# Layer 1's weight factors parked one sum a pair by GpSimd's queue, and another order in the last quad

## The chip, the cores and the metric

The kernel runs on one core of a Trainium2 chip. The metric is the time of one execution on the device, in microseconds; a measurement is the median of several executions. A profiled execution has a span (first to last instruction) beside its own time. The engines are TensorE (PE, with its weight loads PEld), VectorE (DVE), ScalarE (ACT), GpSimd (POOL) and SyncE (SP). Each takes its instructions in the order in which they were built. SP computes nothing here: it issues most of the DMAs; GpSimd issues others and does some elementwise work.

## The reference

A batch of 128 graphs, each with 128 nodes of 512 features, goes through two layers in float32, each of the form x + layer(relu(layernorm(x))).

```python
# layer 0: h = relu(layernorm(x))
Xw = X @ Wv + bv
e = leaky_relu(sj[:, None, :] + si[:, :, None] + ab[0])      # sj, si: Xw times the halves of aw
alpha = A * exp(e)
transition = alpha / (sum(alpha, -1) + 1e-12)
for k in range(3):
    H = H + Xk @ Wk[k] + bk[k]
    Xk = transition @ Xk
return relu(H)
# layer 1: h = relu(layernorm(x))
q, k = split(X @ Wqk);  v = X @ Wv
w = mask / sqrt(512) * sum(q * (adj @ (k * mask)), -1)
return softmax(w, axis=1)[:, :, None] * v
```

Layer 1 needs no q and k of its own: the product of the two halves of Wqk is formed once, so that its score is a product of h, a 512x512 matrix and the aggregate adj @ h. With Wv beside it, its weight is a matrix of 512x1024.

## The kernel before

**Tiling.** The graphs are taken in pairs, p = 0 to 63, in layer 0, and in quads (two pairs), q = 0 to 31, in layer 1. All large products use Strassen's scheme with seven products instead of eight: layer 0 once, layer 1 twice (outer and inner). Its form here (`strassen`, `one_round`) runs products 1, 5, 6, 2, 7, 3, 4 on four PSUM banks a, b, c, e; between them ScalarE copies a to b, e to s, b to c and c to s, and VectorE adds the banks to s. `y10` multiplies by the first two weights of layer 0, `y2` by the third; `inner` and `outer` apply the transition matrix.

**Weight factors.** Layer 1's weight matrix enters as seven outer factors, in the order FACTORS = 1, 5, 2, 6, 3, 7, 4, and each of these as seven inner ones: three are blocks of the outer factor, four are sums, made one from the other. In pairs 5 to 8 `combine_steps(*OUTER)` makes the outer sums, one a pair, each 128x1024. From FIRST = 9 on, `prepare` (lines 653 to 663) makes one factor a pair: four sums of 128x256 on VectorE into the tile `stage`, two ahead of the pair's `begin` and two in the middle of `statistics`, then four stores to the array `rwd` in DRAM, issued by SP behind the store of x1: one with the four sums (512 KB), three with the blocks (128 KB each). After pair 16 the room of the factors' sources (`prep`, `stage`) is given up; the first four factors are read back into it, one a pair, 896 KB each, by SP. The other three are read at the start of layer 1.

**A pair of layer 0.** While PE runs `y10` of pair p and `y2` of pair p + 2, the other engines prepare what comes. SP issues, in order: the store of h (hd) and its read back in blocks (hv), the store of x1 (x1d), the load of x for pair p + 4 (xg), the store of the transition matrix (td) and of the second norm's h (h2d), the read back of td in blocks (junk), and that of h2d (hv). VectorE turns the blocks into transposes: x from hv<-hd, tt from junk, fw from hv<-h2d (line 431). After those follow the pair's x1 (line 625) and its statistics (line 294), then ScalarE's Ln and Exp for it. Behind Exp (`issue_after` of "ln") ScalarE copies y2's first block, then s<-c. GpSimd issues pzd and pz (a column of y2 spread over all partitions through DRAM), fd (the transposed blocks and their sums, 1 MB), and four agb (the adjacency in blocks).

**The order on an engine.** `behind(what, op)` builds `op` so that it stands behind the instruction noted as `done[what]`; `ordered` does that for PE's matmuls. In layer 1 `put` keeps a chain for each engine in the order of the calls.

**The last quad** has its order written by hand in `steps(...)`. The rounds are ra (factors 1 and 2, banks set1), rb (6 and 7, set2), r4 (set1), r5 (set2) and r3 (set1); `(rb, 2)` is rb's third product, p6, with its copy b to c. The others are p1 (0), p5 (1), p2 (3), p7 (4), p3 (5), p4 (6). The tiles s1 and s2 hold the copies of p5. `c[:, 0..3]` are the quad's outputs: scores of the two pairs in 2 and 0, values in 1 and 3. `score` multiplies an aggregate by an output and sums (a SCALAR_TENSOR_TENSOR into junk), `spread_columns_of` turns the scores by PE and takes their maximum (`peaks`), `exp_own` and `exp` form the exponentials on ScalarE, `factors` the quotient, `scale` multiplies the values of an earlier quad, `add_x1` adds x1 to them by a DMA of GpSimd's, `finish` makes the last output and stores it. `p5_of_r5` adds r5's p5 to values 3 and 1 on GpSimd.

Of the kernel before, what the change touches and what calls it, by code (L numbers as in the profile page):

```python
# [9 lines left out]
FP = mybir.dt.float32  # L10
# [6 lines left out]
def kernel(  # L17
# [25 lines left out]
    nc = tc.nc  # L43
# [39 lines left out]
    def behind(what, op, *args, **how):  # L83

        with tc.issue_after(done[what]):
            return op(*args, **how)  # L86
# [6 lines left out]
    def bcast(ap, offset, n):  # L93

        return bass.AP(tensor=ap.tensor, offset=ap.offset + offset, ap=[[0, P], [1, n]])
# [355 lines left out]
    def y2(p, steps={}, gate=None, after="ln"):  # L451


        add = partial(behind, gate, nc.vector.tensor_add) if gate else nc.vector.tensor_add
        y = Y2[p] = front.tile([P, G, 2, WP], FP, name="y2")[:, :, :, :W2]
        s = front.tile([P, 2, WP * 2], FP, name="s", bufs=1)[:, :, :W2]

        def y00(a):
            done["y00"] = behind(after if gate else "warm", nc.scalar.copy, y[:, 0, 0], a).ins

        def y10(c):
            done["y10"] = nc.scalar.copy(y[:, 1, 0], c).ins

        strassen(set2, LEFT[p], right2, s, True, {
            (0, 0): y00,
            (1, 1): lambda e, t: add(y[:, 1, 1], e, t),
            (0, 1): lambda b, t: add(y[:, 0, 1], b, t),
            (1, 0): y10}, steps, seventh="y00")
        if p > 1:

            t = small.tile([P, G, S32], FP, name="pzt", bufs=1)
            behind(gate or "warm", nc.vector.transpose, t, y[:, :, 0, :S32])
            d = dram.tile([G, Q, S32], FP, name="pzd")
            nc.gpsimd.dma_start(d.rearrange("g q b -> q g b"), t[::S32])
            PZ[p] = front.tile([P, G, N], FP, name="pz")
            nc.gpsimd.dma_start(PZ[p].rearrange("p g n -> p (g n)"), bcast(d, 0, G * N))
        else:
            PZ[p] = a2[:, :G * N].rearrange("p (g n) -> p g n", g=G)

# [168 lines left out]
    RWD = {o: dram.tile([P, 7, HD], FP, name=f"rwd{o}", bufs=1) for o in FACTORS}  # L648

    FIRST = 1 + 2 * DC  # L650
    OUTER = ({(kh, k): rl[:, kh * HC:(kh + 1) * HC, k] for kh in range(2) for k in range(2)}, [tl[:, i] for i in range(4)])

    def prepare(o, stage):

        r = {(k, h): rightl[o][:, k, h * HD:(h + 1) * HD] for k in range(2) for h in range(2)}
        t = stage.tile([P, 4, HD], FP, name="stage")

        def store_all():
            behind("x1d", nc.sync.dma_start, RWD[o][:, :4], t)
            for i, at in enumerate(((0, 0), (1, 0), (1, 1))):  # L660
                behind("x1d", nc.sync.dma_start, RWD[o][:, 4 + i], r[at])

        return combine_steps(r, [t[:, i] for i in range(4)]), store_all

    INNER = {5: 0, 6: 1, 7: 2, 3: 3}
    RIGHT = {5: 0, 6: 1, 7: 2, 4: 3, 1: 4, 2: 5, 3: 6}
# [84 lines left out]
    for p in range(NP):  # L751
        weights, weights_end = [], None
        if DC < p <= 2 * DC:
            weights = combine_steps(*OUTER)[p - DC - 1:p - DC]
            weights_end = lambda: rightl.update(combined(*OUTER))
        elif FIRST <= p < FIRST + len(FACTORS):
            weights, weights_end = prepare(FACTORS[p - FIRST], stage)

        def between():
            if p == 0:  # L760
                behind("t", norm0, 2)
                behind("rs", begin, 1)
                return
            if len(weights) > 1:
                for step in weights[:2]:
                    behind("t", step)
            if p + 2 < NP:
                behind("right" if weights else "t", begin, p + 2)
            if p + 3 < NP:
                two = weights[-2:]  # L770
                RS0[p + 3] = behind("left", statistics, xg[p + 3],
                                    middle=(lambda: [behind("aggr", step) for step in two]) if two else None, last="right")

        if p == NP - 1:
            behind("rs2", attention, p)
        def norms():
            if p and p + 3 < NP:
                behind("s7", norm0, p + 3, RS0.pop(p + 3))

        steps = {1: between, 3: norms}  # L780
        if p in T:
            steps[2] = lambda: t_transposed(p)
        if p > 1:
            steps[5] = lambda: masked(p, "ba")
        y10(p, steps)
        if p > 0:
            behind("c12", for_layer1 if p < NP - 1 else SUMS.pop(NQ - 2), *([p - 1] if p < NP - 1 else []))
        if p == NP - 2:
            f0 = w2[:, :8 * G * HC * N].rearrange("p (o j k n) -> p o j k n", o=8, j=G, k=HC)
            load_left(0, swdge)  # L790
        if p == NP - 1:
            for step in inner_sums(0, FACTORS[:4]):
                behind("c12", step)
        z = inner(p)
        if p == 0:
            y2(1, {2: lambda: RS0.update({3: behind("left", statistics, xg[3], "u2")})})
            behind("y10", behind, "hv", norm0, 3, RS0.pop(3))
            spread_columns(1)
            attention(1, lambda: begin(2))
        behind("c12" if p else "left", outer, p, z)  # L800
        if weights:
            weights_end()
        if p + 4 < NP:
            load_x(p + 4)
        if 0 < p <= DC:
            behind("x1d", rows, rl[:, :, 1], wv1, (p - 1,))
        if p == 0:
            setup_ctx.close()
            left = layer0.enter_context(tc.tile_pool(name="left", bufs=1))
            stage_ctx = ExitStack()  # L810
            stage = stage_ctx.enter_context(tc.tile_pool(name="stage", bufs=2, side="right"))
        if p + 2 < NP:
            def ahead():
                attention_exp(p + 1, gate="aggr")
                attention_adj(p + 1)

            def statistics_and_ahead():
                norm2_statistics(p, middle=ahead)
                attention_t(p + 1, "rs2")
                t_by_blocks(p + 1)  # L820

            y2(p + 2, *(({2: statistics_and_ahead}, "t", "z") if p else ()))
        if p + 2 < NP:
            behind("s7", seed_a)
            behind("s7", seed_e)
        elif p + 1 < NP:
            seeds_last()
        norm2(p)
        if p + 3 < NP:
            load_adj(p + 3)  # L830
        if p == FIRST + len(FACTORS):
            stage_ctx.close()
            prep_ctx.close()
            early = ctx.enter_context(tc.tile_pool(name="early", bufs=1, side="right"))
            RW = {o: early.tile([P, 7, HD], FP, name=f"rw{o}") for o in FACTORS[:4]}
        if FIRST + len(FACTORS) <= p < FIRST + len(FACTORS) + 4:
            o = FACTORS[p - FIRST - len(FACTORS)]
            behind("x1d", nc.sync.dma_start, RW[o], RWD[o])
    def left1(q, o, i):
        if i in INNER:  # L840
            return IN[q, o][:, INNER[i]]
# [166 lines left out]
    def exp_own(v, pw, peak):  # L1008
        act(nc.scalar.activation, v[:, 4], v[:, 3], AF.Exp)

    def factors(v, pw, peak):
        dve(nc.vector.reciprocal, v[:, 5], v[:, 2])
        dve(nc.vector.tensor_mul, v[:, 3], v[:, 4], v[:, 5])
# [259 lines left out]
    second_p5()  # L1273
    exp(*soft[2], 3)
    factors(*soft[2])
    exp_own(*soft[0])
    exp(*soft[0], 0)
    steps((rb, 2))
    exp(*soft[0], 1)
    scale(prior, 0, 0)  # L1280
    steps((rb, 3))
# [9 lines left out]
        to = c[:, 1::2, i, j]  # L1291
        return lambda bank, *t: dve(nc.vector.tensor_add, to, bank.to_broadcast([P, 2, HD]), to)

    def p5_of_r5():

        for k in (3, 1):
            pool(nc.gpsimd.tensor_add, c[:, k, :, 1], c[:, k, :, 1], s2[:, 0:1, :HD].to_broadcast([P, G, HD]))

    corners = ((0, 0), (1, 1), (0, 1), (1, 0))
    r4 = one_round(q, set1, (4,), s1, {at: on_s7(*at) for at in corners},  # L1300
                   early=lambda e: in_place(c[:, 0, :, 1])(e.to_broadcast([P, G, HD])))
    r5 = one_round(q, set2, (5,), s2, {at: both(*at) for at in corners}, direct=True)
    r3 = one_round(q, set1, (3,), s1, {at: in_place(c[:, 1:2, at[0], at[1]]) for at in corners},
                   early=lambda e: in_place(c[:, 1, :, 1])(e.to_broadcast([P, G, HD])))

# [4 lines left out]
            op0=OP.mult, op1=OP.add)  # L1310
        queue.dma_start(out[(2 * q + pair) * G + j], r)

    steps((r4, 0), (rb, 5))
    scale(prior, 1, 0)
    steps((r4, 2), (r4, 3), (rb, 6))
    scale(prior, 1, 1)
    add_x1(prior, 1)
    steps((r4, 4), (r5, 0), (r4, 5), (r5, 1), (r4, 1))
    score(1, 0, c[:, 0])
    steps((r4, 6), (r5, 2))  # L1320
    score(1, 1, c[:, 0])
    p5_of_r5()
    for pair in range(2):
        store(late, pair)
    for pair in range(2):
        store(prior, pair)
    steps((r5, 3), (r3, 0), (r5, 4), (r3, 1), (r5, 5))
    soft[1] = spread_columns_of(W[q], a2, G, G)
    exp_own(*soft[1])
    exp(*soft[1], 0)  # L1330
    steps((r3, 2), (r3, 3), (r5, 6))
    exp(*soft[1], 1)
    steps((r3, 4), (r3, 5))
    factors(*soft[1])
    finish(0, 0, c[:, 1, 0], nc.scalar)
# [29 lines left out]
```

## Time and profile before

| | |
|---|---|
| median of 3 executions | 2225.51 us (2223.95 to 2227.53) |
| the profiled execution | 2225.62 us, span 2223.8 us |
| DVE / ACT / POOL busy | 1668.8 / 1236.0 / 697.9 us |
| moved by DMA | 519.35 MB, mean 234 GB/s |
| layer 0, pairs 0 to 62 | about 36.6 to 1408 us of the span |
| last quad | from about 2186 us |

In the lines of the profile a group is named by its line, engine, operation and tiles (out<-in). L91, L86 and L673 are lines of helpers (`ordered`, `behind`, `put`), so that such a line covers many operations; the tiles tell them apart. DVE, ACT, POOL and PE rows are instructions of the engines; SPq and POOLq rows are issues of DMAs. In a timeline the columns are start and length in us, engine, line, operation, tiles, and in brackets the idle time ahead of it with what ended it. In a list of waits they are the waiting instruction, what it waited for, the total in us, the number of waits and the longest one. PE's granted clock was full, 1.00, in every window shown here up to the last few microseconds.

### The profile page before, as it was taken

The numbers are of one execution on the slowest core, as the hardware profiler recorded it, in microseconds if no ns is written. First come the engines' busy times: TensorE is split into PE (matmuls) and PEld (weight loads), VectorE is DVE, ScalarE is ACT, GpSimd is POOL, SyncE is SP. The second block draws the span as 40 slices with busy tenths as digits, with TensorE's granted clock in tenths as the row PEclk, the third lists the DMA queues.
The fourth block names the chain that finished last, engine by engine and source line by source line (L and its number), as shares of the span: only waits on it lengthen the run. The fifth ranks groups of instructions, "written<-read, shape, count | busy, mean of one in ns | idle before, by whom it ended". The sixth has DMA issues, their size and how long they took to land.

```text
span 2223.8 us, 29417 instructions
## 1 busy us (share of the span) xinstructions
PE 2204.0 (99%) x8113; PEld 1535.0 (69%) x8113; DVE 1668.8 (75%) x4532; ACT 1236.0 (56%) x2857; POOL 697.9 (31%) x821
## 2 busy tenths in 40 slices
PE   9999999999999999999999999999999999999998
PEld 6666655666666566666666666688788878887886
DVE  6778777778777777877878777587777767777777
ACT  4555454555455555555555454456666666666664
POOL 2112111212121121212111121255555554555554
PEclk9999999999999999999999999999999999999999
DMA  7688787898788787888778786768888888888876
GB/s 210 202 241 238 226 268 245 272 275 245 228 231 233 225 243 216 245 230 230 239 223 244 217 242 205 264 199 238 229 254 229 233 234 247 236 225 248 235 222 177
DMA packets 425743, 519.35 MB, mean 234 GB/s; under 512 B 100310, under 2 KB 281174, under 8 KB 409706
## 3 DMA queue, kind: packets, MB, share of 16 engines
q1 hardware_dynamic: 384152, 392.36, 58.4%
q0 software_dynamic: 41136, 124.57, 21.5%
q8 instruction: 65, 1.06, 0.2%
q14 instruction: 100, 0.82, 0.1%
q10 hardware_dynamic: 290, 0.53, 0.1%
HBM read 295.26 MB, written 222.07 MB: 233 GB/s over the span
## 4 chain that ended last, share of the span: by engine, by line
PE 90%; DMA 4%; DVE 4%; SPq 1%; issue 1%; ACT 1%; DVEq 0%; ACTq 0%
PE a L91 26%; PE c L91 24%; PE b L91 24%; PE e L91 15%; DMA td<-t 2%; DMA hv<-h2d 2%; SPq L538 1%; DVE st L294 1%; DVE fw L431 1%; SPq L346 0%; DVE x L625 0%; DVE z L86 0%; DMA h2d<-h 0%; DMA xg<-in_x_dram 0%; PE a L284 0%
## 5 line engine op out<-in xcount | busy, mean ns | idle before, releaser
L673 POOL TENSOR_TENSOR c<-s,c 128x512 f32<-128x512 f32 (+1 forms) x186 | 201.1, 1095 | 250.3 <-DVE s L673 245.2
L111 POOL DMA_DIRECT2D agb<-in_adj_dram x256 | 149.8, 592 | 338.3 <-DVE aT L86 246.9
L91 PE MATMUL a<-r,x 128*128 128x512 f32 x512 | 240.8, 592 | 0.0
L91 PE MATMUL b<-rw,in 128*128 128x256 f32 x884 | 212.0, 379 | 0.0
L91 PEld LDWEIGHTS b<-rw,in 128*128 128x128 f32 x884 | 168.0, 190 | 23.3 <-issue 0.5
L439 POOL DMA_DIRECT2D fd<-fw x62 | 34.7, 559 | 470.1 <-DVE fw L447 275.0
L91 PEld LDWEIGHTS a<-r,x 128*128 128x128 f32 x512 | 97.0, 190 | 95.7 <-issue 92.3
L86 ACT COPY s<-c 128x257 f32<-128x257 f32 (+1 forms) x128 | 61.5, 481 | 173.3 <-PE c L91 173.2
L86 ACT COPY b<-a 128x257 f32<-128x257 f32 (+1 forms) x128 | 59.3, 464 | 168.9 <-PE a L91 168.9
L86 DVE TENSOR_TENSOR e<-e,s 128x512 f32<-128x512 f32 x64 | 44.7, 698 | 142.6 <-ACT s L86 142.6
L673 POOL TENSOR_TENSOR c<-c 128x1024 f32<-128x1024 f32 x61 | 144.1, 2362 | 11.2 <-DVE c L673 10.8
L91 PE MATMUL a<-w,x 128*128 128x257 f32 x512 | 131.9, 380 | 0.1
L91 PE MATMUL b<-w,sx 128*128 128x257 f32 x512 | 132.0, 380 | 0.0
L91 PE MATMUL c<-t,sx 128*128 128x512 f32 x256 | 120.5, 593 | 0.2
L91 PE MATMUL e<-t,sx 128*128 128x512 f32 x256 | 120.3, 592 | 0.0
L91 PE MATMUL b<-t,sx 128*128 128x512 f32 x256 | 120.3, 592 | 0.0
L91 PE MATMUL c<-t,x 128*128 128x512 f32 x256 | 120.3, 592 | 0.0
L91 PE MATMUL b<-r,sx 128*128 128x512 f32 x256 | 120.3, 592 | 0.0
L673 DVE SCALAR_TENSOR_TENSOR junk<-agg,wscale,c 128x512 f32<-128x512 f32 x126 | 97.1, 770 | 29.8 <-POOL c L673 24.3
L673 ACT ACTIVATE c<-c,wcol 128x512 f32<-128x512 f32 x124 | 86.3, 720 | 55.7 <-DVE wcol L673 55.7
L431 DVE STREAM_TRANSPOSE fw<-hv 128x256 f32<-128x256 f32 x248 | 88.2, 413 | 34.2 <-DMA hv<-h2d 33.8
L91 PE MATMUL a<-rw,f 128*128 128x256 f32 x448 | 108.1, 379 | 0.0
(265 smaller groups left out, 5256.9 us busy)
## 6 DMA issues: line engine op xcount, KB each, us to landing
fd<-fw POOLq DMA_DIRECT2D x62, 1024.0 KB, 5.1
xg<-in_x_dram SPq DMA_DIRECT2D x64, 512.0 KB, 7.1
x1d<-x SPq DMA_DIRECT2D x64, 512.0 KB, 4.2
h2d<-h SPq DMA_DIRECT2D x64, 512.0 KB, 3.7
hd<-h SPq DMA_DIRECT2D x63, 512.0 KB, 3.6
hv<-hd SPq DMA_DIRECT2D x252, 128.0 KB, 3.9
hv<-h2d SPq DMA_DIRECT2D x248, 128.0 KB, 4.1
h<-h2d SPq DMA_DIRECT2D x62, 512.0 KB, 8.6
```

The source lines that it names most:

```text
L86: return op(*args, **how)
L91: done["mm"] = op(*args, **how).ins
L111: nc.gpsimd.dma_start(agb[p][c * S32:(c + 1) * S32].rearrange("p g q i -> p (g q) i"), v[c])
L294: nc.vector.bn_stats(st, src[:, j, :])
L431: done["c12"] = nc.vector.transpose(blocks[:, k, j].rearrange("p f (n b) -> p f n b", n=Q), hv[:, j].rearrange("p n (k f a) -> p k f n a", ...
L439: nc.gpsimd.dma_start(fd[:, half].rearrange("p o n -> p (o n)"), fv[:, half].rearrange("p o n -> p (o n)"))
L538: done["tv"] = nc.sync.dma_start(tv[c * S32:(c + 1) * S32].rearrange("p g q i -> p (g q) i"), v[c]).ins
L673: done[engine] = op(*args, **how).ins
```

## The change

The sums and stores of the weight factors are spread: each of pairs 9 to 36 makes one sum, in the middle of `statistics`, and stores it (128 KB) and, for three of four sums, one block (128 KB), on GpSimd's queue behind pz, after `y2` instead of behind `outer`. The room is given up after pair LAST = 37, and the first four factors are read back from there in 16 pieces of two inner factors or one, one piece a pair, by GpSimd's queue behind pz. `begin` of pairs 5 to 36 no longer stands behind the sums.

In the last quad: rb's p6 with its copy comes ahead of the exponentials of the first pair's scores; r5's p5 comes ahead of r4's p1 and puts its copy into s1 instead of s2; `p5_of_r5` is taken apart, value 1 ahead of `add_x1(prior, 1)`, value 3 behind r5's p6 and ahead of the last score; r3's p6 with its copy comes ahead of the second pair's exponentials, and r3's p2 and r5's p4 behind both of these.

```diff
             PZ[p] = front.tile([P, G, N], FP, name="pz")
-            nc.gpsimd.dma_start(PZ[p].rearrange("p g n -> p (g n)"), bcast(d, 0, G * N))
+            done["pzq"] = nc.gpsimd.dma_start(PZ[p].rearrange("p g n -> p (g n)"), bcast(d, 0, G * N)).ins
...
+    LAST = FIRST + 4 * len(FACTORS)
+    PIECES = [(o, slice(i, min(i + 2, 7))) for o in FACTORS[:4] for i in range(0, 7, 2)]
...
-    def prepare(o, stage):
+    STAGED = {}
+
+    def prepare(o, i, stage):
 
         r = {(k, h): rightl[o][:, k, h * HD:(h + 1) * HD] for k in range(2) for h in range(2)}
-        t = stage.tile([P, 4, HD], FP, name="stage")
-
-        def store_all():
-            behind("x1d", nc.sync.dma_start, RWD[o][:, :4], t)
-            for i, at in enumerate(((0, 0), (1, 0), (1, 1))):
-                behind("x1d", nc.sync.dma_start, RWD[o][:, 4 + i], r[at])
-
-        return combine_steps(r, [t[:, i] for i in range(4)]), store_all
+        if i == 0:
+            STAGED[o] = stage.tile([P, 4, HD], FP, name="stage")
+        t = STAGED[o]
+
+        def store():
+            behind("pzq", nc.gpsimd.dma_start, RWD[o][:, i], t[:, i])
+            if i < 3:
+                behind("pzq", nc.gpsimd.dma_start, RWD[o][:, 4 + i], r[((0, 0), (1, 0), (1, 1))[i]])
+
+        return combine_steps(r, [t[:, j] for j in range(4)])[i:i + 1], store
...
-        elif FIRST <= p < FIRST + len(FACTORS):
-            weights, weights_end = prepare(FACTORS[p - FIRST], stage)
+        elif FIRST <= p < LAST:
+            o, i = divmod(p - FIRST, 4)
+            weights, weights_end = prepare(FACTORS[o], i, stage)
...
-            if len(weights) > 1:
-                for step in weights[:2]:
-                    behind("t", step)
             if p + 2 < NP:
-                behind("right" if weights else "t", begin, p + 2)
+                behind("t", begin, p + 2)
             if p + 3 < NP:
-                two = weights[-2:]
                 RS0[p + 3] = behind("left", statistics, xg[p + 3],
-                                    middle=(lambda: [behind("aggr", step) for step in two]) if two else None, last="right")
+                                    middle=(lambda: [behind("aggr", step) for step in weights]) if weights else None, last="right")
...
-        if p == FIRST + len(FACTORS):
+        if p == LAST:
...
-        if FIRST + len(FACTORS) <= p < FIRST + len(FACTORS) + 4:
-            o = FACTORS[p - FIRST - len(FACTORS)]
-            behind("x1d", nc.sync.dma_start, RW[o], RWD[o])
+        if LAST <= p < LAST + len(PIECES):
+            o, i = PIECES[p - LAST]
+            behind("pzq", nc.gpsimd.dma_start, RW[o][:, i], RWD[o][:, i])
...
+    steps((rb, 2))
     exp_own(*soft[0])
     exp(*soft[0], 0)
-    steps((rb, 2))
     exp(*soft[0], 1)
...
-    def p5_of_r5():
+    def p5_of_r5(k):
 
-        for k in (3, 1):
-            pool(nc.gpsimd.tensor_add, c[:, k, :, 1], c[:, k, :, 1], s2[:, 0:1, :HD].to_broadcast([P, G, HD]))
+        pool(nc.gpsimd.tensor_add, c[:, k, :, 1], c[:, k, :, 1], s1[:, 0:1, :HD].to_broadcast([P, G, HD]))
...
-    r5 = one_round(q, set2, (5,), s2, {at: both(*at) for at in corners}, direct=True)
+    r5 = one_round(q, set2, (5,), s1, {at: both(*at) for at in corners}, direct=True)
...
-    steps((r4, 0), (rb, 5))
+    steps((r5, 1), (r4, 0), (rb, 5))
     scale(prior, 1, 0)
     steps((r4, 2), (r4, 3), (rb, 6))
     scale(prior, 1, 1)
+    p5_of_r5(1)
     add_x1(prior, 1)
-    steps((r4, 4), (r5, 0), (r4, 5), (r5, 1), (r4, 1))
+    steps((r4, 4), (r5, 0), (r4, 5), (r4, 1))
     score(1, 0, c[:, 0])
     steps((r4, 6), (r5, 2))
+    p5_of_r5(3)
     score(1, 1, c[:, 0])
-    p5_of_r5()
...
     soft[1] = spread_columns_of(W[q], a2, G, G)
+    steps((r3, 2))
     exp_own(*soft[1])
     exp(*soft[1], 0)
-    steps((r3, 2), (r3, 3), (r5, 6))
     exp(*soft[1], 1)
+    steps((r3, 3), (r5, 6))
     steps((r3, 4), (r3, 5))
     factors(*soft[1])
```

More of the change, by code (lines that the diff above doesn't have):

```diff
@@ L800 @@
         behind("c12" if p else "left", outer, p, z)
-        if weights:
-            weights_end()
         if p + 4 < NP:
@@ L822 @@
             y2(p + 2, *(({2: statistics_and_ahead}, "t", "z") if p else ()))
+        if weights:
+            weights_end()
         if p + 2 < NP:
```

## The prediction

> **What bounds the kernel now.** I read the page first, then PE's waits, then windows of equal work, then the queues of one slow pair beside one usual pair, and last the tail.
>
> ```profile
> span 2223.8 us, 29417 instructions
> PE 2204.0 (99%) x8113; PEld 1535.0 (69%) x8113; DVE 1668.8 (75%) x4532; ACT 1236.0 (56%) x2857; POOL 697.9 (31%) x821
> ```
>
> PE is the bound. The change leaves the number of its matmuls alone, so only time in which PE waits or restarts can be won: 2223.8 - 2204.0 = 19.8 us, less what start and end need. PE's waits:
>
> ```profile
> PE c L91 <- ACT s L86: 7.1, 7, 1.5
> PE c L91 <- ACT c L673: 2.5, 2, 2.2
> PE a L91 <- DVE c L673: 1.3, 1, 1.3
> ```
>
> Seven waits of 7.1 us in layer 0 (L86), three of 3.8 us in the last quad (L673). Four windows show where the seven lie: pairs 5 to 8, 9 to 16, 17 to 20, and the eight pairs 26 to 33. Columns: window, length, then busy time and instructions of each engine, clock, DMA share, GB/s.
>
> ```profile
> core 0: us, PE busy (x) PEld busy (x) DVE busy (x) ACT busy (x) POOL busy (x), PEclk, DMA share, GB/s
> 152.10:238.30 86.20, 86.20 (x290) 54.65 (x289) 71.35 (x216) 45.88 (x109) 17.28 (x30) 1.00 0.84 236
> 238.30:421.20 182.90, 175.26 (x577) 108.15 (x576) 138.58 (x443) 92.27 (x217) 31.55 (x55) 1.00 0.83 253
> 421.20:507.40 86.20, 86.20 (x289) 54.52 (x288) 65.62 (x211) 45.96 (x110) 16.60 (x29) 1.00 0.91 275
> 593.60:766.20 172.60, 172.55 (x577) 109.16 (x576) 133.09 (x417) 91.31 (x217) 32.00 (x56) 1.00 0.80 231
> ```
>
> A usual pair takes 21.54 us. Eight pairs with 577 matmuls take 172.6 us in the usual stretch and 182.9 in pairs 9 to 16; against 8 x 21.54 = 172.3 that is 10.6 us lost. Only 7.6 of it is idle time; the rest is in longer matmuls after each wait. Pairs 9 to 15 are those that prepare a factor. Why they are late, SP's queue shows, first around the end of pair 11 (pair 12 begins at 306.17, pair 13 at 329.4), then in a usual pair (the next begins at 550.5):
>
> ```profile
> 325.05 0.38 SPq L627 DMA_DIRECT2D x1d<-x  x1
> 325.47 1.32 SPq L86 DMA_DIRECT2D rwd<-stage  x1
> 326.83 3.51 SPq L86 DMA_DIRECT2D rwd<-tl  x3
> 330.39 0.45 SPq L101 DMA_DIRECT2D xg<-in_x_dram  x1
> 330.94 0.46 SPq L533 DMA_DIRECT2D td<-t  x1
> ...
> 545.10 0.38 SPq L627 DMA_DIRECT2D x1d<-x  x1
> 545.51 1.38 SPq L101 DMA_DIRECT2D xg<-in_x_dram  x1
> 550.59 0.36 SPq L533 DMA_DIRECT2D td<-t  x1
> ```
>
> The four parking stores hold SP for 1.32 + 3.51 = 4.83 us at the pair's end. The load of x, td, and behind them junk<-td (which waits for td) and hv<-h2d start that much later. VectorE shows what comes of it: the transposes that read hv begin at 320.82 in pair 12, 14.65 us after its start, and at 540.60 in pair 22 (start 528.97), 11.63 us after it.
>
> ```profile
> 320.82 1.42 DVE L431 STREAM_TRANSPOSE fw<-hv 128x256 f32<-128x256 f32 x4 [2.27 <-DMA hv<-h2d]
> 540.60 1.43 DVE L431 STREAM_TRANSPOSE fw<-hv 128x256 f32<-128x256 f32 x4 [0.43 <-DMA hv<-h2d]
> ```
>
> These stand ahead of x1 and its statistics on VectorE, whose Ln and Exp stand ahead of ScalarE's copies of y2: the last, s<-c, frees the bank that PE writes next. So the lost time is SP's, a wait and not bandwidth. In the tail, the lines that matter:
>
> ```profile
> 2209.76 1.29 DVE L673 SCALAR_TENSOR_TENSOR junk<-agg,wscale,c 128x512 f32<-128x512 f32 x1
> 2215.24 0.37 ACT L673 COPY c<-b 128x256 f32<-128x256 f32 x1
> 2215.66 0.70 PE L91 MATMUL c<-rw,f 128*128 128x256 f32 x2 [2.21 <-ACT c L673]
> ```
>
> PE waits 2.21 us for a copy of 0.37 us that stands behind exponentials, and a score takes 1.29 us, where the same instruction takes 0.75 at 2190.62.
>
> **What the Trainium skill says.** "DMA: Bandwidth & Descriptors", section "Issuing engines are not separate DMA queues": DMAs of all issuing engines run on the same 16 DMA engines, and spreading the issue saves only sequencer time. The trace agrees that sequencer time is what is short here: 4.83 us of SP, with pairs 17 to 20 moving more bytes (275 GB/s against 253) and losing nothing. "SBUF — State Buffer", section "SBUF: two separate sides": VectorE with two SBUF inputs and GpSimd lock each other out of a shared port pair. The two scores of the last pair, 1.23 and 1.29 us, lie over two GpSimd adds (2207.56 to 2210.50); four others without them take 0.75. The same section warns that a DMA from GpSimd's queue can starve for descriptors beside some VectorE copies; the 256 agb issues (582 to 618 ns, beside VectorE at 75%) show no such case.
>
> **The parking, part by part.** *Off SP:* 28 stores over pairs 9 to 15 and four reads (0.47 us each) in pairs 17 to 20. In the built order SP's, ScalarE's and VectorE's rows of pairs 9 to 36 become those of the usual pairs, but for one sum. That gives back 10.6 us, and nothing is late next: the usual pairs show PE with no gap.
> *On VectorE:* 28 sums of 0.41 us as before, but one a pair between the aggregate and the small operations that wait for ScalarE's Exp. Pairs 5 to 8 hold at that place a sum of 128x1024 at 1.19 us and run 4 x 21.54 us. Cost 0. If the cover were gone: 28 x 0.41 = 11.5 us.
> *On GpSimd's queue:* 49 stores of 128 KB in pairs 9 to 36, 16 reads of 128 or 256 KB in pairs 37 to 52, each about 0.58 us of issue (fd 0.56, pz 0.58). They stand behind pz, which issues at 4.8 us of pair 22; next behind them is fd, whose sums end at 14.8 us. So 1.2 us of issue lies in 9 us of idle queue, ahead of nobody. Cost 0.
> *On the DMA engines:* 0.26 MB a pair, 5% on some 5 MB (231 GB/s x 21.54 us), but landing about 6 to 9 us into the pair, beside junk and hv. If hv waits for all of it at 231 GB/s, it is 1.1 us late: the transposes begin at 12.7 us (even pairs) or 13.4 (odd, usually 12.3). Pair 19 began them at 13.61 and lost nothing to it, pair 10 at 14.0 and lost 0.8. So the load fits, with little to spare in odd pairs. Pairs 17 to 20 read 0.92 MB each, issued 1.9 us into the pair, and lost 0.04 us in all (86.20 against 4 x 21.54). Bounds 0 to 2.5 us (a tenth of a microsecond in half the pairs); I take 0.3, one more stray like that of pair 29 (0.32 us). Sum: -10.3.
> The longer life of prep and stage (to pair 37) asks for no wait: the last store is issued a pair ahead of the first read into their place.
>
> **The last quad.** *The copy c<-b of rb put ahead of exp_own and exp:* PE's wait at 2201.07 (0.28 us, and 0.27 of restart: the four matmuls take 1.13 where four usually take 0.86) goes. But the new place of r5's p5 puts its copy (0.37) ahead of r4's b<-a on ScalarE, which then ends at about 2203.4, where PE's weight load wants it by 2203.16: 0.2 comes back. As p5 itself (0.43) leaves the place ahead of r4's p5, that one ends at 2207.40 - 0.55 + 0.2 = 2207.05, 0.35 earlier; so does VectorE's c<-e behind it, and score(1,0) can begin at 2207.8.
> *GpSimd's adds apart:* the first needs rb's sums (2204.68) and runs 1.27 us to 2205.97; add_x1's issue follows (1.20, to 2207.17), then the second add to 2208.44. It lies over 0.64 us of score(1,0), not over score(1,1). score(1,0) then ends at 2208.8 to 2209.05, c<-c takes 0.35, score(1,1) 0.71: 2209.85 to 2210.1, against 2211.06. I take -1.1. The later add_x1 (0.7 us) delays a store that was issued at 2211.68 and leaves SP long before 2217. PE's transposes wait behind score(1,1) for the next VectorE sum, so they keep the -1.1.
> *r3's copy c<-b ahead of the exponentials:* PE's r3 p7 no longer waits. From wcol (2214.76) to the factors (2217.53) 2.77 us pass now. Then only VectorE's row is left: c 0.33, 0.60, 0.42, 0.43, reciprocal 0.09, product 0.18 = 2.05; the two exponentials end in about 1.0. That is -0.7.
> Sum -1.8; at least -0.8 (the copy costs PE 0.4 more and score(1,0) is locked out longer), at most -2.6 (both scores at 0.75, and the 0.47 us ahead of c<-b at 2213.53 goes).
>
> **Sum.** -10.3 - 1.8 = -12.1. The profiled execution took 2225.62 us (span 2223.8 and 1.8 around it): 2213.5. It stands 0.1 above the median, so 2213.5 stays.
>
> **Rivals.**
> *The tail gives nothing*, because VectorE's rows, which bound it after 2211, are all still there; against it, 2.2 us of that stretch is PE and VectorE waiting for one copy. 2215.3.
> *Part of the stall stays:* hv is 1.5 us late instead of 1.1, odd pairs begin their transposes at 13.8 and lose 0.4 in 14 of the 28: 5.6 us. For it: that place has the pair's thickest traffic. Against: pair 17, transposes at 13.44 behind 0.92 MB, no loss. 2219.
> *Slower:* GpSimd's packets and SP's hv packets alternate on the DMA engines so that hv lands over 2 us late in each of 44 pairs. From 14.0 us on a pair costs 0.8 as pair 10 did; it decides from 12.1/44 = 0.28 us a pair. In the 28 pairs with stores: 28 x 0.8 = 22 us, 2213.5 + 22 = 2235. Against it, the same pairs 17 to 20.
> *It doesn't do what it says:* another wait, say ScalarE's order, set pairs 9 to 16, and they stay slow under another name: about 2224.
>
> **How the numbers follow.** Forecast 0.74, tail nothing 0.08, part stays 0.08, slower 0.05, no effect 0.05. 2211.5 takes the tail's best end and a fast execution (the runs reach 1.6 below their median); 2217.5 takes 2.5 us of strays, the tail's worst end and a slow one. That leaves out the last three, under 0.2. A measurement tells from no change what is over 0.2%, 4.5 us: faster 0.74 + 0.08 + 0.08 = 0.90, same 0.05, slower 0.05.
>
> **What would show it.** Right: the window of pairs 9 to 16 at 172.3 to 173 us, "PE c <- ACT s" gone from PE's waits, rwd under POOL at 0.6 us, pairs 9 to 52 at 21.54; the last score near 0.75 us, PE's wait of 2.2 us gone, about 10.3 us from score(1,0)'s start to the last finish's end (2208.15 to 2219.88 now, 11.7). Wrong: fw transposes beyond 14 us in odd pairs of 9 to 36, or a new wait of PE on tt or s there; in the tail, a score still at 1.2 us or PE waiting for b<-a after r4's p1.

## The result, and the profile after

| | before | after |
|---|---|---|
| median of the runs | 2225.51 us | 2218.66 us (2216.18 to 2220.74, 7 executions) |
| the profiled execution | 2225.62 us, span 2223.8 | 2216.18 us, span 2214.4 |

The ratio is 0.997, with the interval 0.996 to 0.998: faster by 6.85 us, where 12 were forecast. The profiled execution of after is the fastest of its seven; what it shows is 9.4 us of gain.

The head of the page of after:

```profile
span 2214.4 us, 29461 instructions
PE 2201.6 (99%) x8113; PEld 1535.6 (69%) x8113; DVE 1658.0 (75%) x4532; ACT 1235.9 (56%) x2857; POOL 733.2 (33%) x886
```

The same 8113 matmuls as before; PE's busy time is 2.4 us shorter and its idle time 7.0. The windows of after over the profile's pairs 9 to 16, 17 to 37, 38 to 52 and 53 to 62 (columns as in the prediction):

```profile
core 0: us, PE busy (x) PEld busy (x) DVE busy (x) ACT busy (x) POOL busy (x), PEclk, DMA share, GB/s
238.40:410.70 172.30, 172.30 (x577) 109.20 (x576) 133.61 (x422) 91.44 (x217) 38.63 (x68) 1.00 0.80 242
410.70:863.00 452.30, 452.30 (x1513) 286.69 (x1512) 353.27 (x1116) 240.33 (x568) 105.89 (x185) 1.00 0.81 244
863.00:1189.60 326.60, 324.64 (x1081) 204.19 (x1080) 244.25 (x778) 171.59 (x406) 68.19 (x119) 1.00 0.83 239
1189.60:1405.00 215.40, 215.40 (x707) 133.64 (x707) 156.63 (x488) 108.49 (x257) 38.72 (x67) 1.00 0.76 225
```

Pairs 9 to 16 take 172.30 us, the forecast figure: the 10.6 us are back. Pairs 17 to 37, where most of the 49 stores are, take 21.54 us each, and PE is never idle. The third window is new: its 15 pairs should take 15 x 21.54 = 323.1 us and take 326.6. These are the pairs in which the 16 pieces are read back. (What the loop builds on GpSimd's queue in turn p is issued in the profile's pair p + 1, so the reads of turns 37 to 52 stand in pairs 38 to 53; pairs are counted by the profile here.) Of the 3.54 us, pair 42 loses 1.46, pair 38 0.66, pair 48 0.56. PE's waits of after have the same name as before, moved:

```profile
PE c L91 <- ACT s L86: 1.9, 3, 1.2
PE c L91 <- DVE c L679: 1.4, 1, 1.4
PE a L91 <- DVE c L679: 1.0, 1, 1.0
```

Pair 42 begins at 949.93. Its issues by GpSimd and by SP, from the timelines of the two queues:

```profile
954.82 0.59 POOL L476 DMA_DIRECT2D pz<-pzd  x1 [2.88 <-DMA pzd<-pzt]
955.40 0.56 POOL L86 DMA_DIRECT2D rw<-rwd  x1
...
953.53 1.92 SPq L538 DMA_DIRECT2D junk<-td  x4
955.55 1.88 SPq L346 DMA_DIRECT2D hv<-h2d  x4
```

SP is not late: hv is issued 5.62 us into the pair, as in a usual one. But the read of rw is issued 0.15 us ahead of it on the other queue. The list of DMAs of this one pair (KB each and us to landing at the end of an issue's line) shows what that does:

```profile
q1 hardware_dynamic: 4701, 3.01, 49.0%
q0 software_dynamic: 432, 1.57, 23.4%
...
hv<-h2d SPq DMA_DIRECT2D x4, 128.0 KB, 7.2
...
rw<-rwd POOLq DMA_DIRECT2D x1, 256.0 KB, 5.9
```

hv takes 7.2 us from issue to landing; over the whole run its median is 4.4. The first two lines give packets, MB and share of the engines' time: GpSimd's queue (q0) moves about 3.6 KB a packet (1.57 MB by 432), SP's 0.64 KB. Over this window of 22.1 us and 16 engines, a packet of q0 holds an engine for 191 ns (23.4% of 16 x 22.1 us, by 432), one of q1 for 37. Not all of pair 42's lateness is the read's: in two versions below that read nothing there (whole reads by SP, and before with its stores on GpSimd's queue) its transposes begin late as well, at 12.5 us, 0.6 to 0.9 behind those of pairs 44 and 46. VectorE, in pair 42 and then in the odd pair 45, which begins at 1016.00:

```profile
964.35 1.42 DVE L431 STREAM_TRANSPOSE fw<-hv 128x256 f32<-128x256 f32 x4 [3.22 <-DMA hv<-h2d]
965.81 0.69 DVE L446 TENSOR_TENSOR fw<-fw 128x512 f32<-128x512 f32 x1
966.53 0.69 DVE L447 TENSOR_TENSOR fw<-fw 128x512 f32<-128x512 f32 x1
967.14 0.42 DVE L625 SCALAR_TENSOR_TENSOR x<-a,xg 128x256 f32<-128x256 f32 x1
...
1030.76 1.43 DVE L431 STREAM_TRANSPOSE fw<-hv 128x256 f32<-128x256 f32 x4 [2.37 <-DMA hv<-h2d]
1032.11 0.39 DVE L625 SCALAR_TENSOR_TENSOR x<-a,xg 128x256 f32<-128x256 f32 x1
```

The transposes begin 14.42 and 14.76 us into their pairs; pair 42 loses 1.46 us, pair 45 only 0.31. The lines show why: in an even pair two sums of fw (L446 and L447) stand between the transposes and x1, so x1 comes 2.79 us behind the start of the transposes; in an odd pair it comes after 1.35. An even pair has that much less to spare. In the trace of after one rule gives every loss of pairs 38 to 53 within 0.01 us: an even pair loses what its transposes begin past 12.97 us, an odd one past 14.45 (by this rule 3.50 us, lost 3.54). It also gives pairs 10 to 16 of before: 10.20 us by the rule, 10.22 lost. It is fitted to these two traces, and pair 9 of before is outside it: 0.41 us lost with the transposes at 12.72.

In the last quad, VectorE's scores of the second pair and PE's wait of after:

```profile
2200.45 1.32 DVE L679 SCALAR_TENSOR_TENSOR junk<-agg,wscale,c 128x512 f32<-128x512 f32 x1
2202.16 0.75 DVE L679 SCALAR_TENSOR_TENSOR junk<-agg,wscale,c 128x512 f32<-128x512 f32 x1
...
2207.55 0.70 PE L91 MATMUL c<-rw,f 128*128 128x256 f32 x2 [1.39 <-DVE c L679]
```

The last score is at 0.75 us, the copy c<-b no longer ends a wait there, and PE waits 1.39 us for VectorE instead of 2.21 for ScalarE. From the first transpose e<-ident,wcol of the quad to the end of the last finish it is 26.87 us before and 24.80 after: 2.07 won. I call this stretch the tail below. In the nine versions below that keep the new last quad whole it takes 24.54 to 24.79 us, in the two that have the old one whole 26.49.

### The profile page after: what moved, and what is told of

The parts are those of the page before. It is cut to its first block, busy times and chain, and to the rows that moved or that the text cites. A ratio compares the mean times of both kernels' runs of the same rounds, so it can differ in the third digit from the quotient of the medians.

```text
span 2214.4 us, 29461 instructions
## 1 busy us (share of the span) xinstructions
PE 2201.6 (99%) x8113; PEld 1535.6 (69%) x8113; DVE 1658.0 (75%) x4532; ACT 1235.9 (56%) x2857; POOL 733.2 (33%) x886
## 4 chain that ended last, share of the span: by engine, by line
PE 94%; DVE 2%; DMA 2%; SPq 1%; issue 0%; ACT 0%; DVEq 0%
PE a L91 28%; PE c L91 25%; PE b L91 25%; PE e L91 16%; DMA hv<-h2d 1%; SPq L538 0%; DMA td<-t 0%; DVE fw L431 0%; SPq L346 0%; DVE x L625 0%; DVE z L86 0%; DVE c L679 0%; DVE st L294 0%; PE a L284 0%; PE b L284 0%
```

## The experiments

All are versions of after unless said otherwise; "before" in a ratio is the kernel before on the same chip. Questions: do the reads cost because they are whole or in pieces, because of the queue, because of the moment, or by chance; and is the rest of the sum right.

**Whole reads by SP.** Four reads of 896 KB, behind the store of x1 as in before.

```diff
-        if LAST <= p < LAST + len(PIECES):
-            o, i = PIECES[p - LAST]
-            behind("pzq", nc.gpsimd.dma_start, RW[o][:, i], RWD[o][:, i])
+        if LAST <= p < LAST + 4:
+            o = FACTORS[p - LAST]
+            behind("x1d", nc.sync.dma_start, RW[o], RWD[o])
```

> The changed kernel, but the four factors are read back whole (896 KB, one a pair, pairs 37 to 40) by SP behind the store of x1, as in the kernel before. Place (the reads cost because they are issued at 5.4 us of the pair, 0.2 us ahead of hv<-h2d): 2213 to 2214, pairs 38 to 52 at 21.54 us. Queue (GpSimd's packets crowd out SP's hv wherever they stand): the same. Shape (pieces of 2 KB out of rows of 7 KB are slow to read): the same. Chance (pairs are late now and then whatever is read): 2217 to 2219 as the changed kernel, late pairs anywhere.

2213.67 us, ratio 0.9947 (0.9934 to 0.9959). Pairs 38 to 53 lose nothing; a stray of 1.81 us in pair 16 is all. (Pair 16 loses 0.2 to 1.8 us in eight of the twelve versions below that have the change's stores, and nothing in after's trace; whether its stores have a part in it is not shown.) The loss of after is the reads'.

**Whole reads by GpSimd**, behind pz.

```diff
-            behind("x1d", nc.sync.dma_start, RW[o], RWD[o])
+            behind("pzq", nc.gpsimd.dma_start, RW[o], RWD[o])
```

> The changed kernel, but the four factors are read back whole by GpSimd's queue behind pz, in pairs 37 to 40. Place and queue: the four pairs after each read lose 1.5 to 3 us each, with the transposes of hv<-h2d later than 14 us, 2218 to 2224; the other pairs nothing. Shape: nothing lost, 2213 to 2214. Chance: 2217 to 2219, late pairs anywhere.

2225.07 us, ratio 1.0004 (0.9995 to 1.0012): the whole gain is gone in four pairs (3.98, 1.62, 4.97 and 1.11 us). In pair 38 of this run, which begins at 862.43, VectorE's timeline has

```profile
879.30 1.42 DVE L431 STREAM_TRANSPOSE fw<-hv 128x256 f32<-128x256 f32 x4 [4.18 <-DMA hv<-h2d]
```

that is, the transposes at 16.87 us, with hv's reads landing 8.9 to 10.1 us after their issue. The same bytes cost nothing by SP, 3 us earlier in the pair.

**The pieces by SP**, behind the store of x1; they are issued about 2 us into the pair.

```diff
-            behind("pzq", nc.gpsimd.dma_start, RW[o][:, i], RWD[o][:, i])
+            behind("x1d", nc.sync.dma_start, RW[o][:, i], RWD[o][:, i])
```

> The changed kernel, but its 16 pieces are read by SP behind the store of x1 (they come to stand behind h2d, about 2 us into the pair, ahead of junk). Place and queue: nothing lost in pairs 38 to 53, 2213 to 2214. Shape: they lose as in the changed kernel, 3.5 us or more together, 2217 to 2219. Chance: 2217 to 2219.

2213.5 us, ratio 0.995 (0.9936 to 0.9963): what the prediction had forecast for after. In pair 42 (begins at 949.79) the transposes start at 12.53 us, in time:

```profile
962.32 1.42 DVE L431 STREAM_TRANSPOSE fw<-hv 128x256 f32<-128x256 f32 x4 [1.33 <-DMA hv<-h2d]
```

Only pairs 41 and 53 lose anything, 0.17 and 0.23 us, with their transposes on time (12.5 us).

**The pieces on GpSimd's queue, earlier**: behind agb (where `agbq` is noted) and ahead of pz, about 2 us into even pairs or sooner.

```diff
-            behind("pzq", nc.gpsimd.dma_start, RW[o][:, i], RWD[o][:, i])
+            behind("agbq", nc.gpsimd.dma_start, RW[o][:, i], RWD[o][:, i])
```

> The changed kernel, but its 16 pieces are issued by GpSimd's queue behind agb, ahead of pzd or pz, so about 22 us into the pair or 2 us into the next, 3 us or more ahead of hv<-h2d. Place: nothing lost, 2213 to 2214. Queue and shape: they lose as in the changed kernel, 2217 to 2219. Chance: 2217 to 2219.

2214.13 us, ratio 0.995 (0.9938 to 0.9962); in pairs 38 to 53 one stray of 0.22 us. In pair 44, which begins at 994.23, the read is issued 2.01 us into the pair and the transposes begin at 11.96:

```profile
996.24 0.58 POOL L86 DMA_DIRECT2D rw<-rwd  x1
...
1006.19 1.42 DVE L431 STREAM_TRANSPOSE fw<-hv 128x256 f32<-128x256 f32 x4 [0.76 <-DMA hv<-h2d]
```

So GpSimd's queue alone does no harm, and it takes the moment too.

**SP's queue at the bad moment.** The read is built between the reads of td and those of h2d.

```diff
                 t_by_blocks(p + 1)
+                if LAST < p <= LAST + len(PIECES):
+                    o, i = PIECES[p - LAST - 1]
+                    behind("tv", nc.sync.dma_start, RW[o][:, i], RWD[o][:, i])
...
-        if LAST <= p < LAST + len(PIECES):
-            o, i = PIECES[p - LAST]
-            behind("pzq", nc.gpsimd.dma_start, RW[o][:, i], RWD[o][:, i])
```

> The pieces as in the changed kernel, but issued by SP between the reads of td (junk) and those of h2d (hv), at about 5.5 us into pairs 38 to 53: the moment of the changed kernel, on the queue of the reads that were late. If the moment is all that matters (the bytes lie ahead of hv whatever the queue): as the changed kernel, 2216 to 2219 us, 3 us or more lost in pairs 38 to 53, hv landing 6 to 7 us behind its first issue. If it takes GpSimd's queue at that moment as well (its packets served in turn with hv's): 2213 to 2214.5 us, losses under 1 us in those pairs, although hv's issues start 0.5 us later.

2214.01 us, ratio 0.9949 (0.9933 to 0.9966); 0.56 us lost in pairs 39 and 44. SP's queue and VectorE in pair 40, which begins at 907.59:

```profile
913.16 0.45 SPq L86 DMA_DIRECT2D rw<-rwd  x1
913.65 1.91 SPq L346 DMA_DIRECT2D hv<-h2d  x4
...
920.53 1.43 DVE L431 STREAM_TRANSPOSE fw<-hv 128x256 f32<-128x256 f32 x4 [1.75 <-DMA hv<-h2d]
```

The read stands right ahead of hv and pushes its issue to 6.06 us, yet the transposes begin at 12.94 us, 0.03 short of a loss. The test is not quite even: the pieces come one pair later here (39 to 54), so that only four even pairs (40, 44, 48 and 52) read 256 KB, and after has eight. The transposes of these four begin at 12.93 us on average, those of after's eight at 13.35, and those of even pairs that neither read nor store (before, 22 to 60) at 11.78. So the moment alone makes most of the lateness, and GpSimd's queue adds 0.4 us; but that part lies past 12.97, where it costs: 0.05 us a pair here (0.21 in the four), 0.40 in after (3.23 in the eight).

**Shorter rows.** In after's place, each inner factor by a DMA of its own (128 KB, rows of 1 KB like the stores).

```diff
-            behind("pzq", nc.gpsimd.dma_start, RW[o][:, i], RWD[o][:, i])
+            for k in range(i.start, i.stop):
+                behind("pzq", nc.gpsimd.dma_start, RW[o][:, k], RWD[o][:, k])
```

> The changed kernel, its reads at the same place on GpSimd's queue behind pz, but as two DMAs of one inner factor (128 KB in rows of 1 KB) instead of one of two (256 KB in rows of 2 KB): as the stores of pairs 9 to 36 in number, size and rows. Direction (a read into SBUF at that place delays the reads hv<-h2d, a store to DRAM does not): pairs 38 to 53 lose as in the changed kernel, 3 us or more together, 2217 to 2219. Row size (long rows take more than their share of a DMA engine): nothing lost, 2213 to 2214.5.

2216.0 us, ratio 0.9962 (0.9949 to 0.9976); 3.2 us lost in pairs 38 to 50 in its trace, much as in after. In pair 44, which begins at 995.90, the transposes stand at 13.85 us:

```profile
1009.75 1.43 DVE L431 STREAM_TRANSPOSE fw<-hv 128x256 f32<-128x256 f32 x4 [2.65 <-DMA hv<-h2d]
```

The transposes of its even pairs 38 to 52 begin at 13.35 us on average, as in after. The rows do not change the packets: in the traces of both, GpSimd's queue reads the pieces in packets of 4,096 bytes. The median is 2.7 us below after's, but from four and seven executions; what makes that difference stays open.

**Longer rows in the stores.** The version with SP's reads, but with the sums stored two at a time, in rows of 2 KB.

```diff
-            behind("pzq", nc.gpsimd.dma_start, RWD[o][:, i], t[:, i])
+            if i % 2:
+                behind("pzq", nc.gpsimd.dma_start, RWD[o][:, i - 1:i + 1], t[:, i - 1:i + 1])
```

> The kernel e3 (pieces read by SP, 2213.5), but two sums are stored by one DMA (256 KB in rows of 2 KB) in every second pair, with a block's store of 128 KB beside it in half of these. Direction: stores cost nothing, 2213 to 2214.5, no late pair in 9 to 36 above what e3 had (0.35 us). Row size: every second pair of 9 to 36 loses 0.2 to 0.5 us as the reads did, 2216 to 2220.

2213.05 us, ratio 0.9947 (0.9931 to 0.9962), the lowest median measured, though not to be told from 2213.5. The store pairs show no pattern of losses, but that says little: the edit puts the stores of two sums into odd pairs only (11 to 37), where a loss begins at 14.45. The transposes of these pairs begin at 12.8 us on average and 14.02 at the latest; those of odd pairs that read 256 or 384 KB at that place (below), at 13.8 and 15.37.

What decides it is a comparison of the run before this one with after. After's even pairs 10 to 36 store 256 KB each behind pz, in two DMAs with rows of 1 KB, just as the run with shorter rows reads them. With stores the transposes begin at 11.86 to 12.93 us (12.3 on average), with reads at 12.86 to 13.85 (13.35), with neither at 11.78 in before. So stores delay them too, by half a microsecond, and stay short of 12.97; reads delay them by 1.6. The two DMA queues of after over 5 us, from 5.4 us into the pair on, in pair 36 (two stores) and then in pair 48 (one read):

```profile
q1 hardware_dynamic: 1585, 0.55, 42.1%
q0 software_dynamic: 144, 0.39, 32.1%
...
q0 software_dynamic: 128, 0.39, 48.5%
q1 hardware_dynamic: 1216, 0.36, 36.9%
```

GpSimd's queue moves the same 0.39 MB in both (pz is 128 KB of it), in 96 packets of 4,096 bytes and some of 4. But with the read these hold the DMA engines for 48.5% of the time instead of 32.1%, and SP's queue moves a third less. Over all such pairs (18 to 36 and 38 to 52, the even ones) it is 42% against 32%, and 0.41 MB of SP's against 0.54. Why a packet that is read holds an engine longer than one that is stored, no run shows.

**Reads in every second pair.** 12 pieces of three or two inner factors in after's place.

```diff
-    PIECES = [(o, slice(i, min(i + 2, 7))) for o in FACTORS[:4] for i in range(0, 7, 2)]
+    PIECES = [(o, slice(*i)) for o in FACTORS[:4] for i in ((0, 3), (3, 5), (5, 7))]
...
-        if LAST <= p < LAST + len(PIECES):
-            o, i = PIECES[p - LAST]
+        if LAST < p <= LAST + 2 * len(PIECES) and p % 2:
+            o, i = PIECES[(p - LAST) // 2 - 1]
```

> The reads in the changed kernel's place on GpSimd's queue behind pz, the same bytes, but in 12 pieces of three or two inner factors (384 or 256 KB) in odd pairs 39 to 61 only; even pairs read nothing. If an even pair loses what its fw transposes begin past 12.97 us and an odd one what they begin past 14.45 (worked out from the runs so far): at most 1 us is lost in pairs 38 to 61, where one with 384 KB passes 14.45, each by that excess, and the time is 2213 to 2215. If a read costs by its bytes wherever it stands: 3 to 3.5 us lost, all in odd pairs, 2216 to 2219.

They stood in other pairs than the expectation says: the edit puts them in odd turns of the loop, which are the profile's even pairs (40 to 62). 2222.43 us, ratio 0.9984 (0.9976 to 0.9991); pairs 40 to 60 lose 8.65 us, all of it in even pairs, and the odd ones between nothing at all. So I shifted them by one turn:

```diff
-        if LAST < p <= LAST + 2 * len(PIECES) and p % 2:
-            o, i = PIECES[(p - LAST) // 2 - 1]
+        if LAST < p < LAST + 2 * len(PIECES) and p % 2 == 0:
+            o, i = PIECES[(p - LAST) // 2]
```

> The same 12 pieces on GpSimd's queue behind pz, built one pair of the loop away: they are issued in the profile's odd pairs 39 to 61. (In the run before they fell in the profile's even pairs 40 to 62, since what the loop builds in turn p is issued in the profile's pair p + 1; these lost 8.65 us and the odd ones between nothing.) If an even pair loses what its fw transposes begin past 12.97 us and an odd one what they begin past 14.45: the transposes of the odd pairs with reads begin at 13 to 15.5 us, even pairs lose nothing, at most 3 us is lost from pair 38 on, and the time is 2213 to 2216.5. If the bytes cost the same in every pair: again some 8 us, 2220 to 2224.

2215.78 us, ratio 0.9955 (0.9939 to 0.9972). The windows from 863 to 1385 us, first of the version with reads in even pairs:

```profile
863.00:1385.00 522.00, 515.77 (x1713) 324.08 (x1712) 389.07 (x1230) 271.63 (x642) 103.48 (x179) 1.00 0.82 232
```

and then of the one with reads in odd pairs:

```profile
863.00:1385.00 522.00, 520.82 (x1740) 330.21 (x1739) 393.78 (x1251) 275.68 (x650) 103.86 (x181) 1.00 0.80 234
```

In the same time PE does 27 matmuls more. The transposes of the odd pairs begin as late as 15.37 us, but only three pairs lose: 0.92, 0.72 and 0.33 us, each by its excess over 14.45. What a late read costs is set by the pair's free time; how late it is, by the queue and the moment.

**Before with its stores on GpSimd's queue.** The kernel before, its four stores a pair behind pz instead of on SP; the sums still four in one pair.

```diff
-            behind("x1d", nc.sync.dma_start, RWD[o][:, :4], t)
+            behind("pzq", nc.gpsimd.dma_start, RWD[o][:, :4], t)
...
-                behind("x1d", nc.sync.dma_start, RWD[o][:, 4 + i], r[at])
+                behind("pzq", nc.gpsimd.dma_start, RWD[o][:, 4 + i], r[at])
...
-        if weights:
-            weights_end()
...
             y2(p + 2, *(({2: statistics_and_ahead}, "t", "z") if p else ()))
+        if weights:
+            weights_end()
```

> The kernel before, but the four stores of each pair 9 to 15 (0.9 MB) are issued by GpSimd's queue behind pz instead of by SP behind the store of x1; the sums stay four a pair in their old places. If SP's 4.8 us of issue are what made those pairs late, and stores at GpSimd's place cost nothing: pairs 9 to 16 at 21.54 us, 2214.5 to 2215.5. If VectorE's three more sums a pair count as well (4 x 0.41 = 1.6 us): pairs 9 to 15 keep 0.3 to 1 us each, 2217 to 2222. If 0.9 MB of stores at that place delay hv as 0.9 MB of reads did (1.1 to 5 us a pair in e2): 2222 to 2235.

2218.38 us, ratio 0.9976 (0.9967 to 0.9986). Of the 10.6 us some 4.3 stay in pairs 9 to 17. Most of PE's waits there have another name. One of pair 11, from PE's timeline, is

```profile
288.86 1.98 PE L91 MATMUL c<-t,sx 128*128 128x512 f32 x4 [0.41 <-ACT c L86]
```

and the list of waits has them summed over the run (total, number, longest):

```profile
PE c L91 <- ACT c L86: 2.1, 4, 0.9
```

PE waits at y10's product 7. The two sums ahead of `begin` push VectorE in the odd pairs (x transposes at 2.1 us instead of about 0.6), and Ln and Exp, which depend on it, stand ahead of the copy c<-b on ScalarE. These three pairs with sums, 11, 13 and 15, lose 2.04 us; pair 9 loses its 0.41 as in before. The rest is not the sums': pairs 10 and 12 lose 0.69 us with fw transposes at 13.07 and 13.56, beside 0.9 MB of stores each, and pair 17, which makes no sum, loses 1.15 us behind a late read hv<-hd.

**The last quad.** First the version with SP's reads and the whole old last quad (the change's edits there taken back, from `steps((rb, 2))` on).

> The kernel e3 with the last quad's old order: what the new order is worth. From the traces so far (26.87 us before, 24.56 in e3 from the transposes of the first scores to the end of the last finish) 2.3 us slower than e3: 2215.8. By the prediction's sum 1.8: 2215.3. If the old order's late copies were hidden: 2213.5.

2215.21 us, ratio 0.9959 (0.9947 to 0.9972); the tail is 26.49 us against 24.56 in the version with SP's reads: the new order is worth 1.9 us in the traces and 1.7 by the medians. Then two parts undone by themselves, each one execution, read by the tail: r3's p6 back behind the first exponential, and GpSimd's two adds back behind the last score.

```diff
-    steps((r3, 2))
     exp_own(*soft[1])
     exp(*soft[1], 0)
+    steps((r3, 2), (r3, 3), (r5, 6))
     exp(*soft[1], 1)
-    steps((r3, 3), (r5, 6))
```

> The pieces read by SP, with r3's p6 and its copy c<-b back behind the second pair's first exponential; the rest of the last quad as in the changed kernel. Read is the stretch from the first e<-ident,wcol of the last quad to the end of the last finish: 24.55 us with r3's p6 ahead, 26.49 us with the whole old order. If that move is worth what the stretch behind PE's transposes lost (1.28 us, forecast 0.7), PE again waits about 2.2 us for c<-b and the stretch is 25.3 to 25.9 us. If VectorE's row behind wcol bounds it anyway: 24.6.

25.47 us, so 0.91 for this move. PE waits for the copy again, 1.84 us:

```profile
2205.23 0.70 PE L91 MATMUL c<-rw,f 128*128 128x256 f32 x2 [1.84 <-ACT c L679]
```

```diff
-    p5_of_r5(1)
     add_x1(prior, 1)
...
-    p5_of_r5(3)
     score(1, 1, c[:, 0])
+    p5_of_r5(3)
+    p5_of_r5(1)
```

> The pieces read by SP, with both of GpSimd's adds of r5's p5 back behind the last score; the rest of the last quad as in the changed kernel. Same stretch as in the run before, 24.55 us with the adds apart. If the adds apart are what shortened the last score: score(1,1) takes 1.2 to 1.3 us instead of 0.75, PE's transposes begin about 0.5 us later or more than 17.02 us into the stretch, and the stretch is 25.0 to 25.6 us. If the adds don't matter: score(1,1) stays at 0.75 and the stretch at 24.6.

25.17 us, so 0.61 for the adds apart. The last score (the second line) is back at its old length, and PE's transposes start at 17.63 us of the tail instead of 17.02:

```profile
2198.19 1.15 DVE L679 SCALAR_TENSOR_TENSOR junk<-agg,wscale,c 128x512 f32<-128x512 f32 x1
...
2199.72 1.29 DVE L679 SCALAR_TENSOR_TENSOR junk<-agg,wscale,c 128x512 f32<-128x512 f32 x1
```

1.93 - 0.91 - 0.61 leaves 0.4 for rb's p6 and r5's p5, which were not tried alone. Tails of the same order differ by up to 0.25 us between traces, so the parts are good to about that.

## Why the prediction was wrong

- **Failed: "On the DMA engines", taken at 0.3 us, at most 2.5.** The trace shows 3.5 us of it. By medians after stands 5.2 us above the version with SP's pieces (2218.66 against 2213.5; 4.8 when each is set against its own before), and that is the whole miss. Three things in that step were wrong. It priced stores and reads as one load, 49 and 16 alike; beside the stores nothing is lost in after's trace, beside the reads 3.5 us. It took pairs 17 to 20 of before as proof: those reads were on SP's queue and issued at 1.9 us, and neither holds for the change; the run with whole reads on GpSimd's queue behind pz moved the same 0.92 MB and lost 11.7 us in four pairs. And it let hv be 1.1 us late at most, by bytes over a mean rate, where pair 42 has hv at 7.2 us against 4.4.
- **Failed in the same step: how much lateness fits.** "Pair 19 began them at 13.61 and lost nothing to it, pair 10 at 14.0 and lost 0.8" compares an odd with an even pair, and the trace has 0.06 us lost in the one and 1.05 in the other. The bounds are 12.97 and 14.45. The step's own estimate for even pairs, 12.7, was thus 0.27 us from a loss, and it named the odd pairs as the tight ones; 3.23 of after's 3.54 us are in even pairs. The trace of before had it: its pairs 10, 12, 14 and 16 all start past 12.97, and L446 and L447 stand there.
- **The rivals.** "Packets alternate" had the mechanism that fits, but put it in all 44 pairs; "part of the stall stays" had the size (2219), but in the odd pairs with stores, so that its figure is right by luck. "Queues, rings and completion order" of the Trainium skill's page "DMA: Bandwidth & Descriptors" says that each DMA engine takes turns between the queue rows by whole packets. The runs agree as far as they go: with the read on GpSimd's queue SP's queue moves a quarter less in the same 5 us (0.41 MB against 0.54 beside stores), and GpSimd's packets hold an engine five times as long as SP's. On SP's own queue the read goes in packets of 2,048 bytes, and the transposes come 0.4 us earlier. That the packets' turns make this difference is argued from such averages, not shown packet by packet.
- **Right: parking off SP, -10.6.** Pairs 9 to 16 take 172.30 us. But "so the lost time is SP's" was too much: with the stores off SP and the sums left together, 4.3 us remain, of which 2.0 us are shown to come with the sums. The term came out because the change spreads the sums as well.
- **Right: VectorE's sums and GpSimd's issue, 0 each**: pairs 9 to 37 at 21.54 us.
- **Right in size: the last quad, -1.8.** Measured 2.07: up to PE's transposes 0.79 instead of 1.1, behind them 1.28 instead of 0.7. Both profiled executions are unlike most others here. In after's the two adds took 1.69 and 1.50 us and score(1,0) 1.32; in seven of the nine other traces of the new order these are 1.27, 1.26 and 1.07, and the transposes begin 0.25 us earlier. In the trace of before VectorE sat idle for 0.47 us ahead of c<-b at 2213.53; in the two other traces of the old order it is 0.10, so that this gain is not the change's. Between such traces the two parts are 1.0 and 0.9. The sign of 11.7 us, from score(1,0) to the last finish, was taken to 2219.88, while the last finish ends at 2220.54: it is 12.4 before, and 10.7 after.
- **The sum against the profiled execution**: -10.6 + 3.5 - 2.1 = -9.2, and it won 9.4; pairs 19 and 29 of before lose 0.4 us more that after doesn't. The median of after lies 2.5 us above that execution. How late the reads come varies with the execution (the version with reads in even pairs reaches from 2218.69 to 2227.32); that this fills the 2.5 us is argued, since only the fastest was profiled, and strays like that of pair 16 may have a part.

## What to carry to other kernels

Price a background transfer by the transfer it meets, not by the mean rate: its queue, its direction and the moment of its issue decided here between 0 and 12 us for the same bytes. Before saying that a lateness fits, find the last moment that costs nothing, separately for each kind of iteration, from what stands behind the late instruction; two data points from unlike iterations gave a bound that was off by up to a microsecond. Where a loop has room, put such a read where no short-packet read is waited for (here about 2 us into the pair, behind the store of h2d), or in the iterations with more to spare.

## What was not expected of the hardware

- A read of 256 KB on GpSimd's queue, issued beside SP's reads of hv, put the transposes that wait for hv 1.6 us later on average (13.35 against 11.78 us in even pairs); 256 KB of stores in the same place put them 0.5 us later (12.3), though both move in packets of 4,096 bytes.
- The same reads on the same queue some 3 us earlier cost 0.2 us in all, and so did four whole ones of 896 KB on SP's queue.
- The same instructions of the same last quad took different times in different executions: the two GpSimd adds 1.69 and 1.50 us in after's trace and 1.27 and 1.26 in most others, add_x1's issue between them 1.63 and 1.19, and score(1,0) 1.32 and 1.07.
